# Mask products put ahead of the score products in two 16-head attentions

## The chip, the cores and the metric

One Trainium2 chip, of which the program uses one core. The metric is the device time of one execution in microseconds, less is better. A core has five engines that run side by side, each with a queue of its own in program order: TensorE (matrix products, shown as PE, its weight loads as PEld), VectorE (DVE), ScalarE (ACT), GpSimd (POOL) and SyncE (SP, which issues the DMAs here). TensorE writes to PSUM, which has eight banks of 512 fp32 values per partition.

## The reference

The reference is a stack of eight layers on x of 16 x 256 tokens by 128 features, each of the form x = x + layernorm(layer(layernorm(x))). Two of the layers hold the attention that the change is about: the L2 attention (16 heads of 8 features) and the attention half of the L3 layer (16 query heads of 8 features, 4 key heads, each used by four query heads). Cut to that:

```python
# L2 attention: 16 heads, h*d = 128
q = (x @ Wq).reshape(b, t, h, d) * scale
k = (x @ Wk).reshape(b, t, h, d) * scale
v = (x @ Wv).reshape(b, t, h, d)
dot = jnp.einsum('bqhd,bkhd->bhqk', q, k)
dot = jnp.where(causal[None, None], dot, -jnp.inf)
attn = jax.nn.softmax(dot, axis=-1)
out = jnp.einsum('bhqk,bkhd->bqhd', attn, v).reshape(b, t, h * d)
return out @ Wo
# L3 attention: the same softmax, after rms norms and a rotation of q and k,
# with k and v repeated for groups of four query heads
```

Every query sees the keys up to its own place; for 256 tokens and tiles of 128 that makes one triangular block for the first 128 queries, and a full and a triangular block for the last 128.

## The kernel before

The program runs its layers as stages, one after another; each opens its own pools. The 16 sequences are held as eight groups g of 512 tokens (two sequences of 256). Both attentions are run by `attention_stage` (in `stage_l2_attn` and in `l3_gqa`) with the same `attention` generator, once for every group g and each of its two sequences b: 16 calls per stage.

The order of the work is written out by hand. Each part of the work is a generator that yields between its steps. `turns` gives every item a start turn and lets the items advance together; a batch begins every six turns, so that two or three calls of `attention` and the head of a later group (projections, masks of the heads) are always mixed. What is issued in one step goes into each engine's queue in the order of the lines. Within a step the instructions wait only for their data and for their buffers.

PSUM tiles come from rings of banks. In these two stages `RING_BANKS` gives seven banks to the tag "s" and one to "o"; the tags "mm" and "t" are taken from the ring "s" too. So scores, transposed tiles and projections all share seven banks, and a tile's first product waits until the last reader of its bank's former tile is done. Which of the free banks a tile takes is settled when the program is built.

The heads are packed four to a row group: `rows` are four slices of 32 partitions, each with four heads of 8 features. A head's variant v has the other three heads of its row group set to zero (`km`, `qm`, made by `variants`: two copies scaled by a mask on ACT at L382, two on POOL at L383), so that a product over 32 partitions gives the scores of one head. Products over 32 partitions of different row groups run in TensorE's array at the same time.

A call of `attention` goes through three parts:

1. Scores by query (L449 to L461), in three groups, i = 0, 1, 2. Each takes four banks, one for each row group, of 512 columns: four variants by 128 keys for the first query tile (i = 0, "wide" in what follows, as its mask is 512 columns), two variants by 256 keys for the second query tile (i = 1 and 2, "narrow": the mask is on the last 128 keys of each variant, 256 columns). Into each bank go the scores (`km`, `qT`, fp32, in the trace ps_s<-km,qT) and a mask (identity times `negmask`, bf16, ps_s<-b_negmask,b_ident); then DVE takes the negated maximum over the keys (at_nm, L459).
2. POOL splits the maxima in three bf16 pieces (at_pc, L467 and L469), TensorE turns them (L473, ps_s<-b_ident,at_pc), and ACT writes them out as at_mT (L476).
3. Scores by key (L481 to L499), again in three groups of four banks: the products of `kT` and `qm` (ps_s<-qm,kT), the maxima added by ps_s<-at_mT,b_rows, then the exponential on ACT (at_e, L491) and the triangle cut on POOL (L497). The weighted sums with the values follow (ps_o<-at_e,at_vm), the transposes (L525, L537), and the division (L530, L532).

The lines that the change touches:

Of the kernel before, what the change touches and what calls it, by code (L numbers as in the profile page):

```python
# [29 lines left out]
NB, SEQ, P, D = 16, 256, 128, 128  # L30
# [155 lines left out]
def idle(n):  # L186

    for _ in range(n):
        yield


def bc(ap, axis, n):

    ap = ap.unsqueeze(axis)
    shape = list(ap.shape)
    shape[axis] = n
    return ap.to_broadcast(shape)


class Ctx:  # L200
# [233 lines left out]
    def attention(self, g, b, got):  # L434
# [8 lines left out]
        qT, kT, km = (got[n] for n in ("qT", "kT", "km"))  # L443
        ident, negmask, ones = self.cb["ident"], self.cb["negmask"], self.cb["rows"]
# [4 lines left out]
        for i in range(3):  # L449

            t, q, keys, vs = (0, q0, q0, slice(0, 4)) if i == 0 else (1, q1, both, slice(2 * i - 2, 2 * i))
            ss = [self.ps("s") for _ in rows]
            for k, s in zip(rows, ss, strict=True):
                self.mm(s, qT[k, q], km[k, vs, keys], True, False)
            for r, s in enumerate(ss):
                n = vs.stop - vs.start
                s = s.rearrange("p (v n) -> p v n", v=n)
                self.mm(s[:, :, t * P :], ident, bc(negmask, 1, n), False, True)
                v_.tensor_reduce(nm[:, t, r, vs], s, AX.X, ALU.max, negate=True)  # L459
            if i < 2:  # L460
                yield from idle(2)  # L461
# [19 lines left out]
        for i in range(3):  # L481
            vs, to = (slice(2 * i, 2 * i + 2), slice(0, SEQ)) if i < 2 else (slice(0, 4), slice(P, SEQ))
            keys, queries = (q0, both) if i < 2 else (q1, q1)
            ss = [self.ps("s") for _ in range(4)]
# [8 lines left out]
            if i < 2:  # L493
                at, n = e.rearrange("p r (v t n) -> p r v t n", v=2, t=2)[:, :, :, 0, :], 2
            else:
                at, n = e.rearrange("p r (v n) -> p r v n", v=4), 4
# [1574 lines left out]
```

## Time and profile before

| what | value |
|---|---|
| time, median of three runs | 2956.21 us (2953.5 to 2956.53) |
| profiled execution, its own time | 2953.27 us |
| its span, first to last instruction | 2951.5 us |
| mean granted TensorE clock | 0.972 |
| TensorE (PE) busy | 2754.5 us, 93% of the span |
| DVE busy | 1939.0 us, 66% |
| ACT busy | 1670.4 us, 57% |
| POOL busy | 1019.2 us, 35% |
| at_nm<-ps_s on DVE (L459), 384 instructions | 238.0 us busy, 681 ns each; 116.6 us idle before them |
| score products by query, ps_s<-km,qT | 137.4 us over 768 rows, 661 ns each |
| score products by key, ps_s<-qm,kT | 143.6 us over 768 rows, 649 ns each |
| mask products of these lines and others, 256 and 512 columns | 78.9 us over 512 rows, 277 ns each; 35.5 us over 128 rows, 402 ns each |

How to read it. A row of the profile names line, engine and operation, then out<-in by the program's tile names with buffer numbers left out, the shape (partitions x elements and type; 32*128 before a product's shape says that it uses 32 rows and all 128 columns of the array), the number of instructions, their busy time and the mean of one. The products of all helpers have the line L336, so they are told apart by tiles. An fp32 product shows as two rows, one for each pass, and products of different row groups overlap in time, so busy times of rows that overlap are not a sum of time. Idle time of an engine is put down to what ended it. In the timeline a row merges neighbouring instructions of one kind on an engine: start, length from the first start to the last end, engine, line, operation, tiles, count, and in brackets the idle time before it with what released it. All times are microseconds from the start of the span, the means nanoseconds.

### The profile page before, as it was taken

What the parts mean: (1) busy time and instruction counts of PE and PEld (TensorE: products, weight loads), DVE (VectorE), ACT (ScalarE), POOL (GpSimd) and SP (SyncE); (2) the same over time, 40 slices, a digit from 0 to 9 for tenths busy, and PEclk for the clock granted to TensorE, in tenths of its full rate; (3) what the DMA queues carried; (4) which work ended last, traced back from release to release, by engine and by line L of the source; (5) the groups of instructions that cost most, each with busy time, mean ns of one, the idle gap of its engine ahead of it and who ended that gap; (6) DMA issues with size and microseconds to landing.
All of it is one profiled execution on the core that took longest, in us unless ns stands there. A gap on an engine that the chain in (4) does not pass through costs nothing.

```text
span 2951.5 us, 59454 instructions
## 1 busy us (share of the span) xinstructions
PE 2754.5 (93%) x23674; PEld 1875.9 (64%) x23674; DVE 1939.0 (66%) x5309; ACT 1670.4 (57%) x3528; POOL 1019.2 (35%) x1406
## 2 busy tenths in 40 slices
PE   8889999999998699999978998899999799989998
PEld 4557766777666588888853444556656444436897
DVE  5676465564656889999967674666574587736542
ACT  6845556455565567777735665444434377756443
POOL 3553333333336200000044555423221466545332
PEclk9989999999999899999989999899999899999999
DMA  4000000000001000000020000000000000000000
GB/s 117 12 1 2 1 2 2 1 2 1 2 2 38 1 12 12 8 9 8 9 71 5 1 1 1 1 1 1 1 1 1 1 1 1 1 22 37 2 16 16
DMA packets 29150, 31.30 MB, mean 11 GB/s; under 512 B 7292, under 2 KB 20156, under 8 KB 28732
## 3 DMA queue, kind: packets, MB, share of 16 engines
q1 hardware_dynamic: 28872, 27.49, 3.1%
q8 instruction: 187, 3.06, 0.4%
q14 instruction: 91, 0.75, 0.1%
HBM read 23.29 MB, written 4.19 MB: 9 GB/s over the span
## 4 chain that ended last, share of the span: by engine, by line
PE 49%; ACT 7%; DVE 7%; POOL 2%; issue 2%; DMA 0%; POOLq 0%; SPq 0%; ACTq 0%; DVEq 0%
PE ps_s L336 31%; PE ps_o L336 7%; PE ps_mm L336 6%; ACT at_e L491 1%; ACT lg L1199 1%; PE ps_s L325 1%; PE ps_xin L336 1%; ACT meT L1206 1%; PE ps_sum L336 1%; ACT mdisp L1106 1%; ACT lg L1079 1%; PE ps_t L1204 1%; DVE at_nm L459 1%; POOL ln_rs L245 1%; DVE scan L1488 1%
## 5 line engine op out<-in xcount | busy, mean ns | idle before, releaser
L459 DVE TENSOR_REDUCE at_nm<-ps_s 128x2 f32<-128x512 f32 (+1 forms) x384 | 238.0, 681 | 116.6 <-PE ps_s L336 116.6
L491 ACT ACTIVATE at_e<-ps_s 128x512 f32<-128x512 f32 x384 | 198.1, 604 | 94.4 <-PE ps_s L336 92.3
L1488 DVE TENSOR_TENSOR scan<-ps_s,lm 128x384 f32<-128x384 f32 x256 | 124.6, 548 | 142.4 <-PE ps_s L336 142.2
L497 POOL TENSOR_SCALAR_AFFINE_SELECT at_e<-at_e 128x1024 f32<-128x1024 f32 (+1 forms) x96 | 135.1, 1407 | 209.0 <-ACT at_e L491 208.7
L245 POOL TENSOR_TENSOR ln_rs<-ln_rs,mhalf 128x4 f32<-128x4 f32 x192 | 196.2, 1022 | 15.2
L1015 POOL TENSOR_TENSOR ln_rs<-ln_mv,mendt 128x4 f32<-128x4 f32 x6 | 1.2, 199 | 523.5 <-DVE ln_mv L1013 523.5
L336 PE MATMUL ps_o<-my,meT 128*128 128x129 f32 x1024 | 144.3, 289 | 22.1 <-ACT mgot L1218 18.3
L891 DVE TENSOR_REDUCE l_max<-ps_s 128x3 f32<-128x384 f32 x256 | 124.0, 548 | 60.6 <-PE ps_s L336 60.5
L336 PEld LDWEIGHTS ps_s<-l_w,mlp_h 128*128 128x128 f32 x1280 | 149.7, 192 | 20.5 <-issue 15.2
L336 PE MATMUL ps_s<-l1f_phi,mxT 128*128 128x256 f32 x512 | 141.7, 401 | 22.3 <-DVE mpart L1080 16.4
L336 PEld LDWEIGHTS ps_o<-my,meT 128*128 128x128 f32 x1024 | 128.1, 196 | 40.3 <-ACT mgot L1218 23.9
L336 PE MATMUL ps_s<-l_w,mlp_h 128*128 128x128 f32 x1280 | 151.0, 275 | 1.3 <-ACT mlp_h L824 0.9
L336 PE MATMUL ps_s<-qm,kT 32*128 32x512 f32 x768 | 143.6, 649 | 7.5 <-DVE at_nm L459 7.4
L244 POOL TENSOR_SCALAR ln_rs<-ln_mv 128x4 f32<-128x4 f32 x184 | 39.8, 216 | 317.5 <-DVE ln_mv L257 298.9
L336 PE MATMUL ps_s<-km,qT 32*128 32x512 f32 x768 | 137.4, 661 | 11.3 <-DVE qT L1632 3.7
L941 POOL TENSOR_SCALAR_AFFINE_SELECT e<-e 128x512 f32<-128x512 f32 x128 | 78.5, 634 | 172.9 <-ACT e L938 172.9
L336 PE MATMUL ps_o<-at_e,at_vm 128*32 128x128 f32 (+1 forms) x2048 | 123.1, 337 | 15.3 <-ACT at_oT L521 15.3
L336 PE MATMUL ps_mm<-mdisp,mxn 128*128 128x128 f32 x1024 | 126.3, 280 | 4.6 <-DVE mdisp L1118 4.5
L938 ACT ACTIVATE e<-ps_s 128x384 f32<-128x384 f32 x256 | 105.5, 513 | 39.5 <-PE ps_s L336 39.4
L336 PEld LDWEIGHTS ps_mm<-mdisp,mxn 128*128 128x128 f32 x1024 | 122.8, 196 | 7.5 <-DVE mdisp L1118 6.2
L1465 ACT COPY BT<-ps_s 128x512 f32<-128x512 f32 x64 | 37.5, 587 | 158.1 <-PE ps_s L336 158.1
L336 PE MATMUL ps_s<-xT,l_w 128*128 128x512 f32 x256 | 119.7, 597 | 3.8 <-ACT mlp_h L824 2.7
(466 smaller groups left out, 7130.4 us busy)
## 6 DMA issues: line engine op xcount, KB each, us to landing
mw<-in_l1fw SPq DMA_DIRECT2D x16, 256.0 KB, 2.6
moe_w<-in_moe SPq DMA_DIRECT2D x16, 256.0 KB, 5.1
l_w<-in_l SPq DMA_DIRECT2D x10, 256.0 KB, 3.4
x<-in_x SPq DMA_DIRECT2D x8, 256.0 KB, 5.0
xs<-x SPq DMA_DIRECT2D x8, 256.0 KB, 2.1
out<-x SPq DMA_DIRECT2D x8, 256.0 KB, 2.3
slT<-xs SPq DMA_DIRECT2D x6, 256.0 KB, 2.8
l1f_phi<-in_l1f SPq DMA_DIRECT2D x1, 1024.0 KB, 5.1
```

Of the source, the lines that this page charges most:

```text
L244: g.tensor_scalar(out, in_, scale, eps, ALU.mult, ALU.add)
L245: g.tensor_tensor(out, out, self.mhalf[:, :n], ALU.pow)
L325: self.nc.tensor.transpose(out[:n, k * P : (k + 1) * P], src[:, k, cols], self.c["ident"])
L336: self.nc.tensor.matmul(out, lhsT=lhsT, rhs=rhs, start=start, stop=stop, skip_group_check=True)
L459: v_.tensor_reduce(nm[:, t, r, vs], s, AX.X, ALU.max, negate=True)
L491: nc.scalar.activation(e[:, r], s, AF.Exp)
L497: nc.gpsimd.affine_select(at, at, [[0, 4], [0, n], [1, P]], ALU.is_ge, 0.0, base=0, channel_multiplier=-1)
L891: v.tensor_reduce(mx[:, b, :, h, 16], s, AX.X, ALU.max, negate=True)
L938: nc.scalar.activation(e[:, h].rearrange("p j n -> p (j n)"), s[:, : 3 * P], AF.Exp)
L941: nc.gpsimd.affine_select(e[:, :, j, :], e[:, :, j, :], [[0, 4], [1, P]], ALU.is_ge, 0.0, base=0, channel_multiplier=-1)
L1465: nc.scalar.copy(s, ps)
L1488: v.tensor_tensor(m, s[:, : SEQ + P], lm[:, SCAN_HEADS[4 * (t // 2) + 2 * i + hh], :], ALU.mult)
```

## The change

In each of the three groups of part 1, the four mask products are issued first and open the accumulation in their banks; the four score products follow and close it. The four maxima follow as before. A narrow group's mask covers half of the columns of its bank, as before; the other half gets its first value from the score product. Nothing else in the source is changed.

```diff
             t, q, keys, vs = (0, q0, q0, slice(0, 4)) if i == 0 else (1, q1, both, slice(2 * i - 2, 2 * i))
             ss = [self.ps("s") for _ in rows]
+            n = vs.stop - vs.start
+            by_variant = [s.rearrange("p (v n) -> p v n", v=n) for s in ss]
+
+            for s in by_variant:
+                self.mm(s[:, :, t * P :], ident, bc(negmask, 1, n), True, False)
             for k, s in zip(rows, ss, strict=True):
-                self.mm(s, qT[k, q], km[k, vs, keys], True, False)
-            for r, s in enumerate(ss):
-                n = vs.stop - vs.start
-                s = s.rearrange("p (v n) -> p v n", v=n)
-                self.mm(s[:, :, t * P :], ident, bc(negmask, 1, n), False, True)
+                self.mm(s, qT[k, q], km[k, vs, keys], False, True)
+            for r, s in enumerate(by_variant):
                 v_.tensor_reduce(nm[:, t, r, vs], s, AX.X, ALU.max, negate=True)
```

## The prediction

> **What bounds the kernel now.** I read the page first: the engines' shares and the chain that ended last.
>
> ```profile
> PE 2754.5 (93%) x23674; PEld 1875.9 (64%) x23674; DVE 1939.0 (66%) x5309; ACT 1670.4 (57%) x3528; POOL 1019.2 (35%) x1406
> PE 49%; ACT 7%; DVE 7%; POOL 2%; issue 2%; DMA 0%; POOLq 0%; SPq 0%; ACTq 0%; DVEq 0%
> ```
>
> TensorE is the bound and carries most of the chain; the windows view has it busy for 285.0 of 305 us (1525 to 1830, L2 attention) and 287.3 of 310 us (2330 to 2640, grouped-query attention), the two stages that run the changed lines. DVE is busy for 208 and 205 us there. So a DVE delay costs only where TensorE waits for what DVE frees. Next, the at_nm tile (the maxima at L459): what its readers wait for, and who waits for it.
>
> ```profile
>   PE ps_s L336: 116.6, 75
> ...
>   PEld ps_s L336: 28.3, 51
> ...
>   PE ps_s L336: 8.5, 4
> ```
>
> First row: in 75 of 96 groups DVE sits idle until TensorE's product. The other two: TensorE waits 36.8 us for the maxima, because a PSUM bank is free only once its maximum is taken. Last, the timeline of one period (it repeats every 35.2 us) of the L2 stage, and a piece of the second stage:
>
> ```profile
> 1696.23 1.16 PE L336 MATMUL ps_s<-km,qT 32*128 32x512 f32 x8
> 1697.32 0.61 PE L336 MATMUL ps_s<-b_negmask,b_ident 128*128 128x256 bf16 x4
> 1697.64 2.48 DVE L459 TENSOR_REDUCE at_nm<-ps_s 128x2 f32<-128x512 f32 x4 [2.52 <-PE ps_s L336]
> 1697.77 0.28 PE L336 MATMUL ps_s<-b_ident,at_pc 128*128 128x128 bf16 x2
> 1699.78 1.14 PE L336 MATMUL ps_s<-qm,kT 32*128 32x512 f32 x8
> ...
> 1709.25 1.29 PE L336 MATMUL ps_s<-km,qT 32*128 32x512 f32 x8
> 1710.47 1.04 PE L336 MATMUL ps_s<-b_negmask,b_ident 128*128 128x512 bf16 x4
> 1710.90 2.48 DVE L459 TENSOR_REDUCE at_nm<-ps_s 128x4 f32<-128x512 f32 x4 [1.88 <-PE ps_s L336]
> 1712.01 1.36 PE L336 MATMUL ps_s<-qm,kT 32*128 32x512 f32 x8
> ...
> 1717.66 0.18 PEld L336 LDWEIGHTS ps_s<-qm,kT 32*128 32x128 f32 x1 [0.42 <-ACT at_mT L476]
> ...
> 1723.11 0.39 PE L336 MATMUL ps_s<-at_mT,b_rows 32*128 32x512 bf16 x4
> 1723.58 2.06 ACT L491 ACTIVATE at_e<-ps_s 128x512 f32<-128x512 f32 x4 [0.42 <-PE ps_s L336]
> ```
>
> ```profile
> 2469.98 1.14 PE L336 MATMUL ps_s<-km,qT 32*128 32x512 f32 x8
> 2473.08 1.48 PE L336 MATMUL ps_s<-qm,kT 32*128 32x512 f32 x8
> ```
>
> An undisturbed run of four scores (x8: two passes each, in four row tiles at once) is 1.14 us long. What a run is longer by is how late its last bank came: 0.02 at 1696.23, 0.15 at 1709.25, 0.22 at 1712.01 (waiting for a maximum), 0.34 at 2473.08. The first mask follows 1.07 after the start plus that lateness (1696.23 to 1697.32). The x4 row of DVE is the four maxima of a group, 0.68 each and 0.60 apart.
>
> **The change, part by part.** Per group the same eight products run, with the masks first. Nothing is added or removed; DVE, ACT, POOL and SP keep instructions and order (the built programs agree on this), no DMA moves. Four things shift.
>
> *1. The first maximum becomes possible later.* Take P as the group's start. Narrow groups (i = 1, 2; mask of 256 columns), before: masks at P+1.07, maximum 0.32 after the first (1697.32 to 1697.64), so P+1.39. After: four masks at 0.11 (1697.32 to 1697.77) are 0.44, the switch to row tiles 0.09 (between mask and weighted sums the timeline's products stand 0.20 apart, against 0.11 where at_pc follows), the score run 1.14, and the step to its reader. For that step the nearest row is the exponentials behind row-tiled products: 1723.50 to 1723.58, 0.08. That makes P+1.75: +0.36. Wide groups (i = 0): P+1.07+0.43 = 1.50 before; 0.87+0.09+1.14+0.08 = 2.18 after: +0.68. The other maxima follow as now. A rule speaks against the change here: the Trainium skill, "TensorE: Matmul & The Clock Gate", Part 3, "The cost: per-tile semaphore tail", has the increments of concurrent tiles serialize, about 25 + 4.7 per tile + 26.3 per increment ns, 149 ns for four. By that the step is up to 0.15 and the delay +0.43 and +0.75. I take the row, 0.08; had I taken mask to maximum (0.04) the delays were +0.32 and +0.64.
>
> *2. Late banks hide under the masks.* Before, a fourth bank late by L holds all four masks back by L. After, the fourth mask starts at 0.33 (narrow) or 0.65 (wide) anyway, so up to that much of L vanishes from TensorE.
>
> *3. Array modes.* Going between full, row-tiled and column-tiled products costs 0.09. Counted in the built order: 49 groups follow a full-array product of another kind and save a switch, 34 precede one and pay, 4 precede a qm run and save, 6 follow row-tiled products and pay: 1441 switches of the program become 1428, -1.2 us. The skill ("TensorEngine Tiling (Array Packing)", Key Properties) says a mode change drains the array; a mask's result comes 0.16 after its stream (277 ns mean of one, 109 apart), and at 0.16 a switch it would be -2.1. The row decides. For full product to mask I take no switch, as mask to at_pc shows; were there one, up to 49 x 0.09 = 4.4 us more.
>
> *4. Banks.* PSUM tiles of the ring take other banks: 772 of 3109 in the built program. Now a tile of the scores by key (qm,kT) behind at_pc takes at_pc's bank, soon read by at_mT (the 1717.66 row). Then it takes the bank seven tiles back, one of the newest scores, so it needs one maximum more. This is in two of six qm runs per L2 period and three of six in the other stage.
>
> **The sum for an L2 period**, by when the last qm tile starts:
> - Behind 1696.23: needed the third maximum (1699.52, free). Then the fourth: 1700.12 + 0.36 + 0.04 - 0.02 (late bank hidden) = 1700.50 against 1699.80: +0.70.
> - Behind 1702.70: the maxima wait for other DVE work, they start 1705.49, 2.79 after P. No shift: 0.
> - Behind 1709.25: its second maximum is awaited. +0.68, less 0.15 (hidden) and 0.09 (follows a full product): +0.44.
> - Behind 1714.08: 1717.67 now (at_mT). Then the third maximum: 1717.48 (they start at 1715.60) + 0.36 - 0.13 + 0.04 = 1717.75: +0.08.
> - The last two: -0.02 (nothing waits), and 0 (DVE is late by itself).
>
> Together +1.2 us. Behind a waiting qm run on TensorE stand its products with mT and then the weighted sums, and ACT's exponentials (L491) wait for the run; they all move with it, so I take its delay as the stage's. The second stage, period 36.05 us, likewise: behind 2469.98 the fourth maximum at 2473.85 + 0.36 + 0.04 - 0.09 = 2474.16 against 2473.08 + 0.36 = 2473.44: +0.72. Behind the narrow group at 2475.87: 0. Behind the wide one at 2481.58 (late by 0.49, hidden): 0.68 - 0.49 - 0.09 = +0.10. Behind 2486.75 (late by 1.30, of which 0.33 hides): -0.08. Behind 2493.34: -0.02. Behind 2499.01, fourth maximum for a tile that waited for a copy: 2503.10 + 0.68 - 0.11 - 0.09 + 0.04 = 2503.62 against 2503.03: +0.59. Together +1.3 us.
>
> About six full periods in each stage: 6 x 1.2 + 6 x 1.3 = 15.0. Start-up and tail of a stage have fewer waits; I cost them at 0, bound +-1.5 each. Behind the late maxima on DVE's queue stand the reciprocal and at_y (L530, L532), which TensorE transposes over 2 us later (1713.68 and 1716.54): covered; uncovered, 0.4 a period, 5 us. POOL's pieces of nm (L467) move too, but TensorE asks for at_pc over 6 us after them (1709.45 and 1715.73).
>
> The profiled execution took 2953.3 us (span 2951.5): 2968.3 after. It lies 2.9 below the median of the timed runs, 2956.2; against that the forecast is 2971.2. With the step at 0.04 it would be about 2969, with 0.15 about 2974.
>
> **Rivals.**
> - *Faster: the masks fill waits and nobody misses the later maxima.* Hidden lateness and switches alone give 0.5 us per L2 period (0.02+0.15+0.13+0.02+0.11, three switches saved, two paid: 0.52) and 1.2 in the other (0.49+0.33+0.11+0.04, four saved, two paid: 1.15), so 6 x 0.52 + 6 x 1.15 = 10 us less: 2946. For it: ACT and DVE waits reach 1.30 us there. Against: the 36.8 us of TensorE waiting for at_nm. It decides if the qm runs keep their lengths, that is if maxima 0.36 to 0.68 later still come before TensorE.
> - *No change: the moved banks cost nothing,* the extra maximum having come in time. Then 1699.78 gives +0.1, 2473.08 +0.1, 2502.90 0, 1716.88 -0.05 and 2490.71 -0.25, the wide groups keeping theirs: +0.5 and 0 per period, +3: 2959. Against: 1700.12 lies after 1699.78 even without delay.
> - *Much slower: the delay of every group lands,* through DVE's queue and back by the banks: 64 x 0.36 + 32 x 0.68 = 45: 3001. Against: 21 of 96 groups find DVE busy with other work anyway, and most maxima come well before their bank is asked for.
>
> **How the numbers follow.** Forecast 0.80, faster rival 0.06, no change 0.10, much slower 0.04. This kernel's measurement tells about 0.2% (6 us) from no change, so the border to slower is 2962. The forecast's own range is 2964 to 2978 (the step's bounds, start-up, the full-to-mask switch); with the part of the rivals that must be in, 2960 to 2980. Faster 0.06, same 0.09, slower 0.85.
>
> **What would show it.** In the profile after: masks run first; where DVE is free the first maximum starts about 1.22 after its score run (1.14 + 0.08), no longer 0.3 after a mask; score runs are all near 1.14 long, lateness having moved into the mask runs; qm runs behind at_pc grow from 1.14 or 1.5 to about 1.8 to 2.2; TensorE's waits for at_nm rise from 37 to some 70 us, those for at_mT (6.2) vanish. I am wrong if qm runs keep their lengths, or if the two stages change by under 3 us each.

## The result and the profile after

The changed kernel takes 2966.42 us (median of 8 runs, 2962.95 to 2969.62) against 2955.94 us before (8 runs, 2953.5 to 2960.52): 10.5 us more, a ratio of 1.0033 (95% interval 1.0022 to 1.0044). The forecast was 2971.2 us, with a range of 2960 to 2980. The profiled execution after has a span of 2961.1 us, before 2951.5.

In short: with the masks first, the maxima that free the banks start later, and in the moved order of banks some scores by key need one maximum more. TensorE then stops in the middle of a run until that maximum is taken. That costs about 1 us in a period, and about six periods stand in each of the two stages.

The page of the kernel after, engines and the chain that ended last:

```profile
PE 2755.5 (93%) x23673; PEld 1872.6 (63%) x23674; DVE 1933.8 (65%) x5309; ACT 1670.5 (56%) x3528; POOL 1018.2 (34%) x1406
...
PE 49%; DVE 8%; ACT 7%; POOL 2%; issue 2%; POOLq 0%; ACTq 0%; DVEq 0%
```

TensorE's busy time rose by 1.0 us, while the span rose by 9.6: hardly any work was added, waits were. In the chain DVE went from 7% to 8%. Where the waits went shows in the groups by shape (busy time in us and mean in ns of one, then idle time before them and what ended it):

```profile
L336 PE MATMUL ps_s<-qm,kT 32*128 32x512 f32 x768 | 165.7, 644 | 8.3 <-DVE at_nm L461 8.1
...
L336 PE MATMUL ps_s<-km,qT 32*128 32x512 f32 x768 | 113.3, 660 | 2.8 <-DVE qT L1634 1.5 <-POOL km L383 1.3
...
L336 PE MATMUL ps_s<-b_negmask,b_ident 128*128 128x256 bf16 x512 | 83.1, 279 | 11.2 <-ACT at_e L493 6.7 <-DVE at_nm L461 2.0 <-ACT qkv L1581 1.3
...
L336 PE MATMUL ps_s<-b_negmask,b_ident 128*128 128x512 bf16 x128 | 34.4, 388 | 2.6 <-DVE at_nm L461 1.3 <-DVE b_negmask L375 1.2
```

Busy time is here the time covered by at least one product of the group, so a late tile makes a run's busy time longer. (A run is the four products of one kind in a group; a tile here is one bank's product.) The scores by query (km,qT) fell from 137.4 to 113.3 us, as their late banks now hide under the masks (part 2 of the prediction); their mean stayed at 660 ns. The scores by key (qm,kT) rose from 143.6 to 165.7 at an unchanged mean of 644 (649 before): they now wait in the middle of a run. What TensorE's weight loads and products waited for at the tile at_nm (us, times):

```profile
  PEld ps_s L336: 40.7, 86
...
  PE ps_s L336: 11.6, 13
```

Before these were 28.3 in 51 and 8.5 in 4. In the same view for at_mT the 6.2 us of TensorE are gone. The view counts every gap of the weight loads that a maximum ended, also those that cost nothing: in before the first load of the run at 1699.78 has 0.76 put down to a maximum, with products still running until 1699.85. A surer count is that of loads held back inside a run of scores by key, which show as gaps of 0.30 or 0.31 behind at_nm. The traces have 12 of them before and 27 after between 1620 and 1800, in L2, and 0 before and 20 after between 2400 and 2600, in the second stage. The timeline of an L2 period after, a narrow and a wide group with the run of scores by key behind each:

```profile
1700.34 0.61 PE L336 MATMUL ps_s<-b_negmask,b_ident 128*128 128x256 bf16 x4
...
1700.88 1.14 PE L336 MATMUL ps_s<-km,qT 32*128 32x512 f32 x8
...
1702.04 2.48 DVE L461 TENSOR_REDUCE at_nm<-ps_s 128x2 f32<-128x512 f32 x4 [2.81 <-PE ps_s L336]
...
1703.97 1.30 PE L336 MATMUL ps_s<-qm,kT 32*128 32x512 f32 x7
...
1704.58 0.18 PEld L336 LDWEIGHTS ps_s<-qm,kT 32*128 32x128 f32 x1 [0.30 <-DVE at_nm L461]
...
1713.75 1.03 PE L336 MATMUL ps_s<-b_negmask,b_ident 128*128 128x512 bf16 x4
...
1714.70 1.14 PE L336 MATMUL ps_s<-km,qT 32*128 32x512 f32 x8
...
1715.86 2.48 DVE L461 TENSOR_REDUCE at_nm<-ps_s 128x4 f32<-128x512 f32 x4 [2.25 <-PE ps_s L336]
...
1716.35 1.55 PE L336 MATMUL ps_s<-qm,kT 32*128 32x512 f32 x7
...
1717.21 0.18 PEld L336 LDWEIGHTS ps_s<-qm,kT 32*128 32x128 f32 x1 [0.31 <-DVE at_nm L461]
```

A run of scores by key splits in x7 and x1: its last tile is 0.61 late in the first (1703.97 to 1704.58) and 0.86 in the second, each time behind a maximum, as the brackets say (the time in a bracket is the gap between two weight loads, not the lateness). The maxima of the first group begin at 1702.04 and stand about 0.60 apart with 0.68 each, so the fourth ends at 1704.52, and the load at 1704.58 follows it. And of the second stage, two runs and their last tiles:

```profile
2472.56 1.58 PE L336 MATMUL ps_s<-qm,kT 32*128 32x512 f32 x7
...
2473.45 0.18 PEld L336 LDWEIGHTS ps_s<-qm,kT 32*128 32x128 f32 x1 [0.31 <-DVE at_nm L461]
...
2479.56 1.72 PE L336 MATMUL ps_s<-qm,kT 32*128 32x512 f32 x7
...
2480.59 0.18 PEld L336 LDWEIGHTS ps_s<-qm,kT 32*128 32x128 f32 x1 [0.30 <-DVE at_nm L461]
```

An L2 period is now 36.11 us long against 35.19, one of the second stage 37.06 against 36.05: +0.92 and +1.01. Six periods of each at these rates are 11.6 us. Not all of six carry the full rate, though: followed run by run over six periods of each stage (from 1593.4 and 2382.3 in before), the last tiles fall back by 4.9 and 5.7 us, 10.6 together, and 10.3 to 11.1 if one begins a run or two earlier or later. The whole stages, from the last product of the stage in front to the last one with l_wo and l_o, grew by 3.9 and 6.3 us in these two profiles, 10.1 together.

### The profile page after: what moved, and what is told of

Its sections match the earlier page's. It is cut to its first block, busy times and chain, and to the rows that moved or that the text cites. A ratio compares the mean times of both kernels' runs of the same rounds, so it can differ in the third digit from the quotient of the medians.

```text
span 2961.1 us, 59414 instructions
## 1 busy us (share of the span) xinstructions
PE 2755.5 (93%) x23673; PEld 1872.6 (63%) x23674; DVE 1933.8 (65%) x5309; ACT 1670.5 (56%) x3528; POOL 1018.2 (34%) x1406
## 4 chain that ended last, share of the span: by engine, by line
PE 49%; DVE 8%; ACT 7%; POOL 2%; issue 2%; POOLq 0%; ACTq 0%; DVEq 0%
PE ps_s L336 31%; PE ps_o L336 7%; PE ps_mm L336 6%; ACT at_e L493 1%; ACT lg L1201 1%; PE ps_s L325 1%; DVE at_nm L461 1%; PE ps_xin L336 1%; ACT meT L1208 1%; PE ps_sum L336 1%; ACT mdisp L1108 1%; ACT lg L1081 1%; PE ps_t L1206 1%; POOL ln_rs L245 1%; PE ps_s L527 1%
## 5 line engine op out<-in xcount | busy, mean ns | idle before, releaser
L336 PE MATMUL ps_s<-qm,kT 32*128 32x512 f32 x768 | 165.7, 644 | 8.3 <-DVE at_nm L461 8.1
L336 PE MATMUL ps_s<-b_negmask,b_ident 128*128 128x256 bf16 (+1 forms) x640 | 117.5, 300 | 13.7 <-ACT at_e L493 6.7
L336 PEld LDWEIGHTS ps_o<-at_e,at_vm 128*32 128x32 f32 x2048 | 45.7, 109 | 122.9 <-issue 106.6
```

What stands on the lines that cost most here:

```text
L336: self.nc.tensor.matmul(out, lhsT=lhsT, rhs=rhs, start=start, stop=stop, skip_group_check=True)
```

## The experiments

Theory: the loss is the waiting for maxima, and it needs both parts, the later maxima and the banks that moved with the order. Rivals: the order alone, the banks alone, or a cost of masks-first products that has nothing to do with the maxima.

To take order and banks apart, the banks of the two stages are given as strings, one digit for each tile of the ring, with the order of the source untouched. The names of the lines move down by 19 in these kernels (L355 is the products' line, L478 or L480 the maxima's).

```diff
+RINGS = {
+    "l2a": "0615234061523406152340615423064125306412530...",
+    "l3g": "0651243065124130264153026415302641530421653...",
+}
...
     def ps(self, tag):
...
+        if tag == "s" and self.ring:
+            tag, self.ring = "s" + self.ring[0], self.ring[1:]
+            return self.psum.tile([P, 512], F32, tag=tag, name="ps_s", bufs=1)
```

### The control: the program of before, with strings

The edit is only the one above, with the banks of before.

> A control: the order and the banks of before, built with the strings of banks that the other runs use; each engine gets the instructions and waits of before. It tells what part of the other runs' times lies in how they fell and not in their edit. Theory (start-up and tail of a stage move by some us with the half-speed stretches of TensorE's clock, whatever the edit): within 3 us of before in the median, steady periods equal to 0.02 us, but the profile's start-up and tail may differ by up to 5 us together with the TensorE time at half clock (36.6 us in the two stages before). Rival (building with strings costs by itself): 3 to 5 us slower in the median.

Measured: 2957.26 us against 2957.43, ratio 0.9999 (0.9991 to 1.0007). The steady periods agree with before to 0.02 us (at the start of the second stage's one run comes 0.06 earlier, and the next has made it up). The profile's first stage is 3.6 us longer all the same, and 3.4 of that arise between 25 and 60 us after its beginning. The windows view of before, then of the control, over the same part of the stage, which begins 4.06 us later in the control (length, busy time of PE, PEld, DVE, ACT, POOL, then the granted clock, the DMA share and GB/s):

```profile
1558.00:1566.00 8.00, 6.22 (x41) 3.15 (x43) 6.89 (x19) 3.94 (x9) 5.94 (x12) 1.00 0.11 34
1566.00:1572.00 6.00, 5.67 (x38) 2.29 (x34) 5.75 (x18) 4.92 (x13) 4.99 (x5) 1.00 0.00 0
```

```profile
1562.00:1570.00 8.00, 5.91 (x27) 1.85 (x30) 6.13 (x14) 1.84 (x4) 5.40 (x9) 0.57 0.12 34
1570.00:1576.00 6.00, 6.00 (x38) 2.82 (x31) 4.10 (x15) 4.93 (x11) 3.07 (x7) 1.00 0.00 0
```

The same instructions were granted full clock here in one profile and 0.57 over the first 8 us in the other: the control's records have one stretch of 6.83 us at half clock more, and half of it is 3.4 us. So a profile's steady periods can be compared to hundredths of a us, and a stage's start-up and tail only to some 4 us. In what follows the steady periods tell what order and banks cost; the medians tell what a whole execution costs.

### Order and banks apart

First the old order with the new banks, then the new order with the old banks.

> Scores first, masks second, as before; only the PSUM banks of the ring in the two attentions are set by hand to those that the changed program took. Theory (late maxima and moved banks share the cost): the qm run behind the first narrow group now needs the fourth maximum at its old time, so about +0.4 us in an L2 period and +0.4 in a period of the second stage, 6 periods each, less what at_mT no longer holds up: +3 to +9 us. Rival 1 (the order alone): 0, within 2 us. Rival 2 (the banks alone): all of it, +10.

> Masks first, as changed; the banks are set by hand to those that the program before took. Theory: the maxima are 0.36 or 0.68 us later, but fewer qm runs need the newest ones: +2 to +7 us. Rival 1 (the order alone): +10. Rival 2 (the banks alone): 0 or, as late banks hide under the masks, down to -10.

Measured: banks alone 2962.69 against 2956.36, ratio 1.0023 (1.0014 to 1.0032), +6.3 us, within the expected 3 to 9; order alone 2963.76, ratio 1.0028 (1.0017 to 1.0039), +7.4 us, just above the expected 2 to 7. How much later than before the last tile of each run of scores by key starts, by item (the increase over the item before it, in us; starts of before name the items):

```text
L2 stage, behind       1696.23  1702.70  1709.25  1714.08  1719.50  1724.59   period
predicted                +0.70     0       +0.44    +0.08    -0.02     0       +1.20
after                    +0.67   -0.19     +0.37    +0.06     0        0       +0.92
order alone              +0.09     0       +0.37    -0.03     0        0       +0.43
banks alone              +0.38   -0.19     +0.19    -0.12     0        0       +0.26

second stage, behind   2469.98  2475.87  2481.58  2486.75  2493.34  2499.01   period
predicted                +0.72     0       +0.10    -0.08    -0.02    +0.59    +1.31
after                    +0.68   -0.11     +0.03    -0.13     0       +0.55    +1.01
order alone              +0.08   -0.11     +0.03    -0.22     0       -0.05    -0.27
banks alone              +0.48     0        0       -0.12     0       +0.14    +0.50
```

(Entries are rounded one by one, so a row can miss its sum by 0.01.) In the first and the last column the parts do not add: 0.09 and 0.38 make 0.67, -0.05 and 0.14 make 0.55. There the moved bank asks for one maximum more, and this maximum is also later. With the banks alone the run behind at_pc already shows it, at a place where before had 1.14 (the timeline of the old order with the new banks):

```profile
1701.80 1.52 PE L355 MATMUL ps_s<-qm,kT 32*128 32x512 f32 x8
```

In the column 1709.25, on the other hand, order alone costs all of it. On average over both kinds of period that is +0.97, of which the order alone makes 0.08 and the banks alone 0.38: more than half is the meeting of the two. Neither rival of one part alone holds in the steady periods. The medians do not show this meeting: 6.3 and 7.4 us add up to more than 10.5, where 6 x (0.43 - 0.27) = 1.0 us is all that the order alone costs at its steady rates. So that kernel was run again.

> The same program as new_order_old_banks, whose +7.4 us lay for only some 1.5 us in the twelve steady periods. If its rest is a property of the program's start-up and tail: again +6 to +9, with start-up and tail of both stages longer in this trace too. If it came from how that profile and those runs fell: the profile's start-up differs by some us from the first one's, and the ratio lies apart from 1.0028.

Measured: 2963.81 us against 2959.61, ratio 1.0012 (1.0006 to 1.0019), +4.2 us: the two intervals barely touch. The profile repeats the first to 0.2 us in its stages (7.4 and 4.0 us longer than before). Both profiled executions are slow ones, 4.3 and 3.5 us above the medians of their kernel, while that of before is 2.7 below its own. From the first product to the last of each stage, 56.3 us of TensorE's busy time lie at half clock, against 38.6 before, 45.5 in the control and 39.2 after (the expectation of the control has 36.6, by other bounds of the stages). Up to half of such time is lost, so 17.7 us more can make up to 8.9 of the 10.4 us by which the stages grew beyond the steady rates. That is an estimate from the clock records; why this program meets more half-clock stretches in both profiles is not settled, nor how the 4 to 7 us of its medians divide.

### Wide or narrow groups alone

Old banks, and the masks first only in the wide groups (i = 0) or only in the narrow ones.

```diff
...
+            first = i == 0        # the other kernel: i > 0
+            if first:
+                for s in by_variant:
+                    self.mm(s[:, :, t * P :], ident, bc(negmask, 1, n), True, False)
             for k, s in zip(rows, ss, strict=True):
-                self.mm(s, qT[k, q], km[k, vs, keys], True, False)
+                self.mm(s, qT[k, q], km[k, vs, keys], not first, first)
...
+                if not first:
+                    self.mm(s[:, :, t * P :], ident, bc(negmask, 1, n), False, True)
                 v_.tensor_reduce(nm[:, t, r, vs], s, AX.X, ALU.max, negate=True)
```

> Masks first in the wide groups only (i = 0), scores first in the narrow ones, old banks. Theory: the wide groups have the longer delay (0.68 against 0.36) and the qm run behind them waits for their second maximum: nearly all of what the new order costs with old banks, +3 to +7 us. Rival (every group's delay costs in proportion to its length, 32 x 0.68 of 45): about half of it, +1 to +3.

> Masks first in the narrow groups only (i = 1, 2), old banks. Theory: their 0.36 us fits before the bank is asked for, and late banks hide under the masks: -3 to +1 us. Rival (every group's delay costs in proportion): half of the order's cost, +1 to +4.

Measured: wide 2960.70 against 2956.36, ratio 1.001 (1.0004 to 1.0017), +4.3 us; narrow 2957.82, ratio 1.0006 (0.9998 to 1.0014), no difference that can be told from 0 and not the gain that was hoped for. The steady periods (L2, then the second stage): wide +0.37 and -0.02, narrow -0.05 and -0.25. So in these, with the old banks, the wide groups in L2 cost all that there is (their maxima come 0.6 later and one of them is awaited), while the narrow ones gain a little by hidden lateness and a saved switch. At these rates six periods of each make +2.1 and -1.8 us; what the medians have beyond that, 2.2 and 3.3 us, lies outside the steady periods, like the excess of the order alone, and stays open like it.

### Shorter maxima: does the sign turn?

If the waits for maxima are the cause, maxima that are done in time must leave only what the change gains. These two kernels take each maximum over the first half of its variant's keys only, one with order and banks of before, one with those of the change. The exponentials' shift is then the maximum of half of the keys; nothing else is changed.

```diff
-                v_.tensor_reduce(nm[:, t, r, vs], s, AX.X, ALU.max, negate=True)
+                v_.tensor_reduce(nm[:, t, r, vs], s[:, :, : (64 if i == 0 else P)], AX.X, ALU.max, negate=True)
```

> Order and banks of before; each maximum is taken over the first half of the keys of its variant only (64 of 128 in the wide groups, 128 of 256 in the narrow ones), so that a reduction reads 256 columns of its bank and takes some 0.35 us in place of 0.68. Theory (TensorE waits for maxima because their banks come free late): the waits for at_nm in TensorE's view, 36.8 us before, nearly vanish, and the kernel is 5 to 15 us faster than before. Rival (the banks and the array modes cost by themselves, whatever the maxima do): below 3 us faster.

> Masks first and the banks of the changed kernel, with the same half maxima. Theory: the maxima now come before TensorE asks for their banks, although they still start 0.36 to 0.68 later; so nothing is left of the delay, only the lateness hidden under the masks and the switches saved, 10 us by the sum of the faster rival, and the waits of qm runs for at_mT are gone too: 5 to 15 us FASTER than short_maxima_old. Rival (masks first or the moved banks cost by themselves): slower than short_maxima_old by some 10 us, as with whole maxima. Between (-3 to +3): half maxima are still late in part.

Measured, same chip: 2950.23 us with order and banks of before, 2928.88 with those of the change, the kernel before 2959.61. The ratios to it are 0.9968 (0.9955 to 0.998) and 0.9895 (0.988 to 0.991), so that the change now gains 21 us where it lost 10. Both kernels have the same shorter maxima, so what differs between them is order and banks alone. The sign turns, and the gain is larger than the 5 to 15 expected. (The second kernel is a probe and no replacement: a key in the other half can exceed the shift.) The timeline of the second kernel (group, maxima, run behind it):

```profile
1703.68 0.61 PE L355 MATMUL ps_s<-b_negmask,b_ident 128*128 128x256 bf16 x4
...
1704.22 1.14 PE L355 MATMUL ps_s<-km,qT 32*128 32x512 f32 x8
...
1705.38 1.42 DVE L480 TENSOR_REDUCE at_nm<-ps_s 128x2 f32<-128x256 f32 x4 [1.12 <-PE ps_s L355]
...
1706.45 1.19 PE L355 MATMUL ps_s<-qm,kT 32*128 32x512 f32 x8
```

Four maxima take 1.42 us (415 ns each) instead of 2.48, and the run behind them is x8 in one piece. That TensorE's waits for at_nm would nearly vanish did not come true as a sum: the tile's view still has 24.8 us with the old order and 29.9 with the new. But 15.0 and 16.0 of these are one stop in the start-up that stands in two rows, and of the loads held back for 0.30 or 0.31 inside a run none is left in either kernel, between 1620 and 1800 as between 2400 and 2600, against 12 before and 47 after. The gain per period between the two kernels is 1.42 us in L2 and 1.85 in the second stage, against 0.52 and 1.15 in the sum of the faster rival. Two things are more than in that sum. With short maxima and the old order the runs of scores by query were later than before (1.83, 1.35, 1.35 and 1.25 us for the late ones of an L2 period), so there was more lateness to hide, and all are 1.14 in the new order. And the waits of a last tile for at_mT (0.79 late once in an L2 period, 0.78 and 0.35 in the second) are gone with the moved banks. What the prediction counted as a gain is real; whole maxima eat it up.

### Banks by hand

The last question is whether the later maxima can be avoided by the banks. Here each tile gets the bank whose former tile was read out first by the traces' times, for both orders.

> Masks first, whole maxima; in the two stages every tile takes the bank whose former tile was read out first, by the times that the traces show, in place of the bank that the pools pick. Theory (a later maximum costs only through the bank that a waiting tile was given): most of the waits for at_nm can be avoided by giving a tile of the scores by key another bank, so the loss of 10 us shrinks to between -3 and +3 us against before. Rival (masks first cost by the later end of DVE's chain, whatever the banks): +6 to +10, as after.

> The order of before with banks chosen in the same way. Theory: before's own waits for at_nm and at_mT in the steady periods (some 2.7 us of late last tiles in an L2 period, 1.5 in the other) shrink, 3 to 6 us faster than before, and faster than new_order_free_banks by some 3 us, since its maxima can start 0.3 to 0.6 earlier. Rival: no measurable change, since the lateness is hidden again elsewhere (exponentials, POOL's triangles).

Measured: masks first 2957.67 us against 2956.70, ratio 1.0006 (0.9998 to 1.0014); old order 2958.24, ratio 1.0001 (0.9993 to 1.001). So with masks first the choice of banks takes away all but some 1 us of the loss, as the theory has it, and the rival's +6 to +10 is out. The old order did not get faster by the expected 3 to 6 us. Its steady periods are shorter, by 0.38 and 0.12 us (3.0 over six of each; masks first: 0.25 and 0.27, 3.1), but the rest of the stages is some 7 us longer than before's in both profiles, with 56.2 us at half clock in the old order and 48.4 in the new one. In the medians (+1.5 and +1.0 us) the same sum leaves 4.5 and 4.1 us beside the steady periods; what they come from was not tested. Neither of the two kernels beats before by what can be measured.

## Why the prediction was right, and by how much it was off

The direction, the mechanism and the places were right; the size was 4.5 us too large (+15.0 forecast, +10.5 measured), of which 3.4 lie in the rate of the steady periods (15.0 against 11.6 for six of each) and about 1 in their count (11.6 against the 10.6 that the runs of six periods show).

- *Part 1, later maxima.* Right, but the step from the run of scores by query to its first maximum was mis-sized. I took 0.08 from the exponentials; from the start of a score run to the maximum it is 1.16 in the narrow and in the wide group above (1700.88 to 1702.04, 1714.70 to 1715.86), with a run of 1.14: a step of 0.02. The other row, mask to maximum with 0.04, was nearer, and the rule of the Trainium skill, "TensorE: Matmul & The Clock Gate", Part 3, "The cost: per-tile semaphore tail", with up to 0.15 lay further off. So the delays were 0.30 and 0.62, not 0.36 and 0.68. (The end of a product is modelled in these profiles, so the 1.16 is surer than its split.) At three items in each kind of period the delay lands: 12 x 3 x 0.06 = 2.2 us of the overshoot.
- *Part 2, hidden lateness.* Right: both runs of scores by query shown are 1.14 long, and 24 us left the row km,qT.
- *Part 3, switches.* The mask run to the score run takes 0.54 and 0.95 (1700.34 to 1700.88, 1713.75 to 1714.70), 0.53 and 0.96 by my 0.44 + 0.09 and 0.87 + 0.09. Nothing shows a switch in front of a mask.
- *Part 4, banks.* Right: the moved banks make 0.38 of the 0.97 by themselves, and 0.89 once the maxima are later (0.97 less the 0.08 of the order alone).
- *Two items costed at 0.* Behind 1702.70 the period became 0.19 shorter, in after and with the banks alone, and not with the order alone. The prediction said that the maxima wait there for other DVE work; that work itself waits for POOL's triangle, which follows the exponentials, and these follow a last tile by 1.41 us if the four tiles start together (1699.80 to 1701.21) and by 1.23 if it is late (1704.58 to 1705.81). So 0.18 of each late tile at this place does not reach the next one. Behind 2475.87 the change gives 0.11, with masks first alone and not with banks alone: transposes by the full array stand in front (ps_s<-const_ident,rot, at 2475.28 before), so a switch of 0.09 is saved, which the rival's sum had and this item had not. Six periods of both: 1.8 us of overshoot. With the 2.2 of the step that is 4.0; the remaining items were forecast too low by 0.1 in an L2 period and the second stage's together, 0.6 in six. The exponentials named, before and then after:

```profile
1701.21 2.06 ACT L491 ACTIVATE at_e<-ps_s 128x512 f32<-128x512 f32 x4 [0.74 <-PE ps_s L336]
```

```profile
1705.81 2.06 ACT L493 ACTIVATE at_e<-ps_s 128x512 f32<-128x512 f32 x4 [1.14 <-PE ps_s L336]
```

- *Start-up and tail at 0.* What lies outside six periods at the full rate came to -1.5 us in these two profiles (10.1 against 11.6), -0.5 if the runs are followed one by one (10.6). That this is near 0 is in part luck of the clock. Near the end of the L2 stage before has a stretch of 3.41 us at half clock that after lacks (the last runs of scores by key lose 1.6 of their delay there), and near the end of the second stage after has one that before lacks (+1.6, last section). At the start of the L2 stage the first maxima come 3.89 us after the projection in front of them begins (1538.03 to 1541.92) and 3.07 before, but the granted clock between 1536 and 1540 is 0.52 after and 0.78 before, and 2.43 and 2.38 were measured in the two profiles of the order alone. So what the change itself does there cannot be told from these profiles.
- *TensorE's wait for at_nm "37 to some 70".* It went to 52.3, and the runs of scores by key behind at_pc did grow to lengths of 1.75 to 2.2 (last tile's lateness plus 1.14), as forecast. I had read the 36.8 wrongly: the waits view lists the longest wait last in each row, and in before one wait stands in both rows.

```profile
PE ps_s L336 <- DVE at_nm L459: 8.5, 4, 7.1
```

```profile
PEld ps_s L336 <- DVE at_nm L459: 27.0, 43, 7.9
```

The 7.1 and the 7.9 are one stop in the start-up (its load is recorded at 1578.78), so some 15 of the 36.8 us were never waits of the steady periods. A stop of that kind is in after too (7.4 and 8.2), so 15 to 16 of the 52.3 are no more than that either.

The rivals: *faster* fell, although its 10 us exist, as the short maxima show. It named the point that decides: whether maxima come before TensorE asks. *No change* put the cost of the moved banks at nothing; with the banks alone they cost 0.38 of the 0.97 a period. *Much slower* had no sign in any run.

## What to carry to other kernels

When two products fill a bank, putting the longer run last makes the bank's reader start later (here by 0.30 and 0.62 us). This costs only where someone waits for the bank next: look at the run behind, and at which maximum its last tile needs, rather than at the sum of waits. A change of order under a ring of buffers also changes who follows whom in each buffer: list both, and test them apart by writing the assignment out. Compare steady periods between profiles, item by item: in whole stages the stretches of half clock, which differ between runs of one program, come on top.

## What the runs showed of the hardware

The granted clock has only the values 1.0 and 0.5 in the records, in stretches of multiples of 3.41 us (but for the one in which a record ends), and where they fall differs between runs of one program. After the same stop of 2.8 us near the end of the second stage, before went on at full clock and after did not. The windows, and the first run of products behind the stop, of before and then of after:

```profile
2628.00:2632.00 4.00, 4.00 (x48) 1.51 (x47) 0.84 (x3) 2.06 (x4) 1.32 (x2) 1.00 0.00 0
```

```profile
2640.00:2643.00 3.00, 3.00 (x28) 1.01 (x20) 0.21 (x1) 2.01 (x4) 0.00 (x0) 0.60 0.00 0
```

```profile
2628.43 1.14 PE L336 MATMUL ps_s<-qm,kT 32*128 32x512 f32 x8
```

```profile
2638.66 1.84 PE L336 MATMUL ps_s<-qm,kT 32*128 32x512 f32 x8
```

The run took 1.84 us in place of 1.14, and from the end of the stop to the next run of scores by key it is 5.16 us instead of 3.58. The Trainium skill, "TensorE: Matmul & The Clock Gate", Part 1, "What's actually happening", describes a free-running window of 3413 ns, which agrees with the records.

The other surprise is a DVE instruction that takes five times its length beside POOL. First before, then after:

```profile
1703.35 2.01 POOL L497 TENSOR_SCALAR_AFFINE_SELECT at_e<-at_e 128x2048 f32<-128x2048 f32 x1 [3.67 <-ACT at_e L491]
1703.41 2.16 DVE L1388 TENSOR_SCALAR lm<-lm,dt 128x384 f32<-128x384 f32 x1
```

```profile
1707.94 2.01 POOL L499 TENSOR_SCALAR_AFFINE_SELECT at_e<-at_e 128x2048 f32<-128x2048 f32 x1 [4.15 <-ACT at_e L493]
1708.19 1.98 DVE L1390 TENSOR_SCALAR lm<-lm,dt 128x384 f32<-128x384 f32 x1
...
1724.20 0.39 DVE L1390 TENSOR_SCALAR lm<-lm,dt 128x384 f32<-128x384 f32 x1
```

With POOL at work on the triangle, this row lasts until 0.21 to 0.22 after POOL's end (1705.36 to 1705.57, 1709.95 to 1710.17); alone it takes 0.39. In the L2 stage all the long ones (1.97 to 2.24 us, 7 of 16 in each profile) overlap such a triangle and all the short ones (0.39 to 0.42) do not. The skill's page "SBUF — State Buffer", "Terms", has a port pair that DVE and GpSimd hold as an exclusive lock for a whole instruction, the other being blocked; these rows fit it, and no run here tested it by itself. For this kernel it is why the maxima behind 1702.70 hang on POOL and not on TensorE.
